# Places of their own for three of the steps that end a chunk, in slots 8 to 20 of a convolution, attention and experts kernel

## The chip, the core and the metric

The kernel runs on one core of one Trainium2 chip. The metric is the device time of one execution in microseconds. Before the change three executions took 3090.45, 3093.17 and 3100.2 us; the median is 3093.17 us.

The core has five engines with an instruction stream each: TensorE (PE, with its weight loads PEld), VectorE (DVE), ScalarE (ACT), GpSimd (POOL) and SyncE (SP, which issues most of the DMAs). [...]

## What is computed

The input is x of 8 images of 56 by 56 pixels with 256 channels, 8 x 3136 tokens in all. Three blocks follow each other (cut to what matters):

```python
# layer 0: 32 bottleneck paths, 256 -> 4 -> 3x3 -> 4 -> 256 channels, each with batch norm and relu
paths = vmap(_path)(x, W1, ..., V3)
x = relu(paths.sum(axis=0) + x)
# layer 1: attention without softmax; t has 8 heads of 32 channels
q = layernorm(t).heads
k = v = (q - mean) / (std(q, ddof=1) + 1e-5)      # per token and head
out = q @ (k.T @ v / N)                           # k.T @ v is 32 x 32, summed over all tokens of the image
t = t + out + layernorm(t)
# experts: top 2 of 8, gelu MLP 256 -> 256 -> 256
t = t + sum over e of combine[e] * (gelu(layernorm(t) @ w1[e] + b1[e]) @ w2[e] + b2[e])
```

What matters here is the middle: after the convolution of a chunk of tokens, their means and deviations per head are taken, the tokens are divided by the deviations, and the product k.T @ v is added to a sum that needs all chunks of its image before its attention can begin.

## The kernel before

**Chunks and slots.** The tokens are cut into S = 56 chunks of 448 (seven for each image), each laid out as 4 tiles of 112 tokens. The program is one long loop over slots. In slot s the heavy third convolution of chunk s runs, and woven into it are the lighter steps of other chunks: the first convolution of chunk s+2, the second of chunk s+1, the end of chunk s-1 (`end_steps`), and from slot A = 8 on the attention of chunk s-8. Routing of tokens to experts, the scattering of the routed rows to DRAM and the planning of expert tiles come with it. Expert tiles run from slot 18 on: a few in slots 18 to 20, and about as many as fit from slot 21 on, when the second plan is known (`known_in[1]` is 21).

**The third convolution** is 32 pairs a slot (`pair`): two matmuls into two PSUM banks (L660), a relu of the one on ACT into the tile `r` (L665), and a maximum and sum with the other on DVE (L668). A place of the order holds two such pairs; I call them PAIR0, PAIR2, ... PAIR30 by the number of the first. Two places, four pairs, make a unit, whose four `r` tiles are then summed over paths by TensorE (L681, `sum_paths`); these sums are SUM0 to SUM7, and SUM7 falls into the next slot. SUM5 takes the tiles of PAIR20 and PAIR22. Seven PSUM banks serve all matmuls but these sums, which have one bank, so that a pair may start only when ACT or DVE has read the banks of earlier ones.

**The end of a chunk** has ten steps: `begin` (relu, transposed copy to DRAM), `turn` twice (transposition on TensorE), `means` (DVE), `center` (POOL), `squares` (ACT), `variances` (ten DVE instructions, and at their end, L801, a power on POOL that turns variances into deviations), `inverse` (three DVE instructions, L814, L818, L823: the reciprocals of deviations, which read what the power wrote), `scale` (two POOL multiplications, L827), and `products` (16 matmuls, L837, and one DVE addition of the result, L845, or a copy, L843, in an image's first chunk).

**The order is written by hand.** PE, ACT and DVE execute in the order in which the program issues; POOL and SP are ordered when the program is built, by what is ready. `places` gives each step a place between 0 and 1 within the slot. `at` pairs steps with places, and `issue` sorts all steps of a slot by place and calls them. The third convolution is spread evenly over 0 to 1: a place of two pairs has weight 0.7 and a sum 0.9, together 18.4, so that PAIR22, which has 11 pair places and 6 sums ahead of it, stands at (7.7 + 5.4 + 0.35) / 18.4 = 0.731. In the same way PAIR20 stands at 0.644, SUM4 at 0.688, PAIR24 at 0.769, SUM5 at 0.812, PAIR26 at 0.856, PAIR28 at 0.894 and SUM6 at 0.938. Other steps near them are the second half of the second convolution with `halves` (DVE L340 and L342) at 0.675, the attention's writes of normalised rows on ACT (0.689, 0.744, 0.798, 0.881), its additive step on POOL (L1060, at 0.94) and, in slots with a plan (16 and 19), `runs` at 0.726 and `members` at 0.783, both on DVE.

Slots before 8 take the places of "end alone". All later ones up to 55 take those of "end".

Of the kernel before, what the change touches and what calls it, by code (L numbers as in the profile page):

```python
# [25 lines left out]
def kernel(  # L26
# [42 lines left out]
    A = NCH + 1  # L69
# [187 lines left out]
    def is_chunk(s):  # L257
        return 0 <= s < S
# [9 lines left out]
    def conv1_steps(s):  # L268
        b, c = divmod(s, NCH)
        xT = xtp.tile([P, NF, CH], F32, tag="xT", name=f"xT_{s}")  # L270
        xTs[s] = xT

        def turn(f):
            X = xs_in[s]
            tp = ps_mm.tile([P, 512], F32, tag="mm", name=f"tx_{s}_{f}")
            for k in range(KT):
                nc.tensor.transpose(
                    tp[:, k * T : (k + 1) * T], X[:, k, f * P : (f + 1) * P], ident[:T, :T]
                )
            nc.scalar.copy(xT[:, f, :], tp[:, :CH])  # L280

        def product():
            del xs_in[s]
            if is_chunk(s + 1):
                load(s + 1)
            ps = ps_mm.tile([P, 512], F32, tag="mm", name=f"c1_{s}")
            for f in range(NF):
                nc.tensor.matmul(
                    ps[:, :CH], W1s[:, f, :], xT[:, f, :], start=(f == 0), stop=(f == NF - 1)
                )  # L290
            nc.scalar.activation(
                h1[:, 1 + c * ROWS : 1 + (c + 1) * ROWS, 1 : HW + 1],
                ps[:, :CH].rearrange("p (r w) -> p r w", w=HW),
                AF.Relu, bias=sh1, scale=sc1,
            )

        return [(0.5, lambda: turn(0)), (0.5, lambda: turn(1)), (1.6, product)]
# [4 lines left out]
    def spread_taps(s):  # L302

        b, c = divmod(s, NCH)
        R = taps.tile([3 * 32, NG, TL], F32, tag="R", name=f"R_{s}")
        flat = h1.rearrange("p r w -> p (r w)")
        r0 = c * ROWS * W58
        for dx in range(3):
            n = TL - dx
            queue = nc.scalar if s == 0 and dx == 1 else nc.sync  # L310
            queue.dma_start(
                out=R[dx : 3 * 32 : 3, :, :n], in_=flat[:, r0 + dx : r0 + dx + n]
            )
        tapped[s] = R
# [174 lines left out]
    def center_router():  # L489
        tp = ps_mm.tile([P, 512], F32, tag="mm", name="tp_rw")  # L490
        for f in range(NF):
            nc.tensor.matmul(tp[:, :E], mean_of, rwc[:, f, :], start=(f == 0), stop=(f == NF - 1))
        for f in range(NF):
            nc.vector.tensor_sub(rwc[:, f, :], rwc[:, f, :], tp[:, :E])
# [109 lines left out]
    def unordered(ins, group, keep=()):  # L604
# [23 lines left out]
        "conv2": [0.621, 0.658, 0.658, 0.675],  # L628
        "conv2 alone": [0.531, 0.629, 0.629, 0.806],
        "end": [0.109, 0.151, 0.244, 0.244, 0.337, 0.431, 0.551, 0.681, 0.761, 0.908],  # L630
        "end alone": [0.121, 0.156, 0.166, 0.226, 0.306, 0.386, 0.386, 0.636, 0.73, 0.865],
        "fetch": [0.103],
        "image": [
# [58 lines left out]
    def conv3_steps(s):  # L692
        steps = []
        units = NF * NQ
        for step in range(0, 4 * units, 2):
            if is_chunk(s):
                steps.append((places["conv3"][0], lambda step=step: (pair(s, step), pair(s, step + 1))))
            if step == 0 and is_chunk(s - 1):
                steps.append((places["conv3"][1], lambda: sum_paths(s - 1, units - 1)))
            if step and step % 4 == 0 and is_chunk(s):  # L700
                steps.append((places["conv3"][1], lambda step=step: sum_paths(s, step // 4 - 1)))
        return steps
# [270 lines left out]
    def fetch(a):  # L973
        ts, tTs, us = spilled.pop(a)
        X = attn.tile([T, KT, C], F32, tag="X", name=f"X_{a}")
        tT = attn.tile([P, NF, CH], F32, tag="tT", name=f"tT_{a}")
        nc.sync.dma_start(out=tT, in_=tTs)
        nc.sync.dma_start(out=X, in_=ts)
        for n in range(2):
            nc.sync.dma_start(  # L980
                out=totals[a % 2][32 * n : 32 * n + 2, :].bitcast(F32), in_=us
            )
        fetched[a] = tT
        Xs[a] = X
# [541 lines left out]
    def at(name, steps):  # L1526

        out, last = [], 0.0
        for place, (_, fn) in zip(places[name], steps, strict=True):
            last = max(last, place)  # L1530
            out.append((last, last, [(0.0, fn)]))
        return out
# [20 lines left out]
    def tiles_by(s):  # L1553


        most = known_after[-2] - 2
        after = [int(v) for v in places["after"]]
        if s >= S:
            return most - sum(after[s - S + 1 :])
        begin, end = known_in[1] - 1, S - 1  # L1560
        at_hand = known_after[0] - 2
        return at_hand + (most - sum(after) - at_hand) * (s - begin) // (end - begin)


    def put_off(m):

        return m % NCH == NCH - 1 and m + 1 + A < S

    known_in = [
        m + A + 1 + (1 if m >= S - NCH else 2) + (1 if put_off(m) else 0) for m in closing  # L1570
    ]
    r, upto = -1, -2
    waiting, left = [], []
    for s in range(S + A + 1):
        a = s - A
        work_of = []
        era = " alone" if s < A else ""
        if s <= S:
            work_of.append((0.0, 1.0 if is_chunk(s) else 0.1, conv3_steps(s)))
        if is_chunk(s + 2):  # L1580
            work_of.extend(at("conv1" + era, conv1_steps(s + 2)))
        if is_chunk(s + 1):
            work_of.extend(at("taps" + era, [(0.0, lambda: spread_taps(s + 1))]))
            work_of.extend(at("conv2" + era, conv2_steps(s + 1)))
        if is_chunk(s - 1):
            if s < S:
                work_of.extend(at("end" + era, end_steps(s - 1)))
            else:
                work_of.append((0.12, 0.99, end_steps(s - 1)))
        if is_chunk(a + 1):  # L1590
            work_of.extend(at("fetch", [(0.0, lambda: fetch(a + 1))]))
        if is_chunk(a):
            opens = a % NCH == 0
            if opens:
                work_of.extend(at("image", image_steps(a // NCH)))
            if a + A > S:
                work_of.extend(at("attention first last" if opens else "attention last", attn_steps(a)))
            else:
                work_of.extend(at("attention first" if opens else "attention", attn_steps(a)))
        work_of.extend(left)  # L1600
        left = []
        group = waiting
        if waiting and put_off(waiting[0]):
            group = [] if waiting[0] == a - 1 else waiting[:1]
        if group and (len(group) == 2 or group[-1] % NCH == NCH - 1):
            last_image = group[-1] >= S - NCH
            compute, scatters = route_steps(group)
            rt = places["route" if s < S else "route last"]
            work_of.append((rt[0], rt[1], compute))
            if last_image:  # L1610
                work_of.append((places["scatter last"][0], 0.995, sum(scatters, [])))
            else:
                work_of.append((places["scatter"][0], 0.995, scatters[0]))
                left = [(0.0, places["scatter"][1], steps) for steps in scatters[1:]]
            if group[-1] in closing:
                work_of.append((places["plan"][0], places["plan"][1], plan_steps(closing.index(group[-1]))))
            waiting = waiting[len(group) :]
        while r + 1 < len(closing) and known_in[r + 1] <= s:
            r += 1
        if r >= 0 and r + 1 < len(closing):  # L1620
            goal = upto + (known_after[r] - 2 - upto) // (known_in[r + 1] - s)
            if r + 2 < len(closing):
                goal = min(known_after[r] - 2, goal if s < known_in[1] else tiles_by(s))
            work_of.append((places["tiles"][s <= known_in[r]], places["tiles"][2], moe_steps(upto, goal)))
            upto = goal
        if s == 1:
            center_router()
        if 1 <= s <= E:
            work_of.append((0.5, 0.5, [(0.0, lambda: copy_weights(s - 1))]))
            work_of.append((0.8, 0.8, [(0.0, lambda: empty_rows(s - 1))]))  # L1630
        if s == S + 1:
            apart.append(s)
        issue(*work_of)
        if is_chunk(a):
            waiting.append(a)
# [60 lines left out]
```

## Time and profile before

| what | us |
|---|---|
| three executions, median | 3093.17 |
| the profiled execution, from outside | 3074.19 |
| its span, first to last instruction | 3072.3 |
| PE busy | 2842.7 |
| DVE busy | 2143.1 |
| ACT busy | 1915.4 |
| POOL busy | 1798.8 |

The profile is of one execution, and all durations below are of that one. It was 19 us quicker than the median of the three; 1.9 us of it lie outside the span. The mean granted clock of TensorE was 0.968.

PE is busy for 93% of the span, but the share isn't even. The page's rows of 40 slices show it at 8 tenths in the part from about 307 to 845 us, which is that of slots 8 to 19 (slices of 76.8 us), and at 9 from there on. By the first matmul of the third convolution, slots start as follows.

| slot | starts at us | lasts us |
|---|---|---|
| 8 | 307.0 | 47.9 |
| 9 | 354.9 | 40.0 |
| 10 | 394.8 | 45.8 |
| 11 | 440.6 | 37.7 |
| 12 | 478.3 | 44.0 |
| 13 | 522.3 | 37.7 |
| 14 | 560.0 | 44.2 |
| 15 | 604.2 | 47.0 |
| 16 | 651.2 | 48.5 |
| 17 | 699.7 | 45.7 |
| 18 | 745.5 | 38.7 |
| 19 | 784.2 | 51.9 |
| 20 | 836.1 | 44.2 |

Slots 8 and 15 open an image's attention, 16 and 19 make a plan, and 10, 12, 14, 16, 17 and 19 route and scatter. A view of stretches gives each engine's busy time in such a window and the granted clock of TensorE; a view of the timeline gives the instructions in order with the idle time ahead of each and what ended it, in square brackets.

### The profile page before, as it was taken

What the parts mean: (1) busy time and instruction counts of PE and PEld (TensorE: products, weight loads), DVE (VectorE), ACT (ScalarE), POOL (GpSimd) and SP (SyncE); (2) the same over time, 40 slices, a digit from 0 to 9 for tenths busy, and PEclk for the clock granted to TensorE, in tenths of its full rate; (3) what the DMA queues carried; (4) which work ended last, traced back from release to release, by engine and by line L of the source; (5) the groups of instructions that cost most, each with busy time, mean ns of one, the idle gap of its engine ahead of it and who ended that gap; (6) DMA issues with size and microseconds to landing.
All of it is one profiled execution on the core that took longest, in us unless ns stands there. A gap on an engine that the chain in (4) does not pass through costs nothing.

```text
span 3072.3 us, 54367 instructions
## 1 busy us (share of the span) xinstructions
PE 2842.7 (93%) x16901; PEld 1649.8 (54%) x16901; DVE 2143.1 (70%) x5705; ACT 1915.4 (62%) x3859; POOL 1798.8 (59%) x1333
## 2 busy tenths in 40 slices
PE   7999888888899999999999999999999997898898
PEld 3334443334455555555555555555555555786687
DVE  6777878888777877787877877787778775453100
ACT  4666566556666676667766667667666664554355
POOL 2332245444565766757766666676664656677677
PEclk9999899989999999999999999999999998998899
DMA  3555445436477778677777877778877766998897
GB/s 102 145 118 131 113 141 137 130 103 183 122 179 190 172 200 209 164 199 188 195 193 176 207 175 190 195 176 206 193 167 185 182 175 147 230 278 215 208 215 172
DMA packets 373233, 538.19 MB, mean 175 GB/s; under 512 B 91488, under 2 KB 283344, under 8 KB 372944
## 3 DMA queue, kind: packets, MB, share of 16 engines
q1 hardware_dynamic: 289984, 430.49, 49.7%
q0 software_dynamic: 82368, 103.47, 20.3%
q8 instruction: 135, 2.21, 0.3%
q14 instruction: 154, 1.26, 0.2%
q10 hardware_dynamic: 592, 0.76, 0.1%
HBM read 248.42 MB, written 192.75 MB: 144 GB/s over the span
## 4 chain that ended last, share of the span: by engine, by line
PE 39%; DVE 4%; DMA 3%; ACT 3%; POOL 3%; issue 3%; POOLq 0%; ACTq 0%; DVEq 0%; SPq 0%
PE ph L1447 8%; PE py L1467 7%; PE c L660 6%; PE su L681 6%; DMA out_dram<-y,index 3%; PE te L1403 2%; PE py L1463 2%; PE at L1010 2%; PE c L324 2%; PE kv L837 1%; POOL regions L1191 1%; DVE r L668 1%; ACT r L665 1%; POOL out_dram L1485 1%; ACT y L1471 1%
## 5 line engine op out<-in xcount | busy, mean ns | idle before, releaser
L668 DVE SCALAR_TENSOR_TENSOR r<-c,nb,r 128x448 f32<-128x448 f32 x1792 | 1127.2, 676 | 379.1 <-ACT r L665 374.9
L665 ACT ACTIVATE r<-c,b3t 128x448 f32<-128x448 f32 x1792 | 1037.0, 634 | 340.7 <-PE c L660 334.5
L660 PE MATMUL c<-hl,W3hl 64*128 64x448 f32 x3584 | 700.7, 430 | 36.4 <-ACT r L665 19.8
L1191 POOL DMA_INDIRECT regions<-pay,rrowi x448 | 428.0, 955 | 300.0 <-PE c L660 181.5
L1485 POOL DMA_INDIRECT out_dram<-y,rows x258 | 408.0, 1582 | 318.4 <-ACT y L1471 243.1
L660 PEld LDWEIGHTS c<-hl,W3hl 64*128 64x128 f32 x3584 | 331.2, 188 | 488.9 <-issue 215.5
L681 PE MATMUL su<-r,gather 128*32 128x448 f32 x3584 | 540.5, 566 | 43.4 <-DVE r L668 33.6
L1471 ACT ACTIVATE y<-py,rows 128x256 f32<-128x256 f32 x420 | 195.9, 474 | 468.2 <-PE py L1467 348.0
L1447 PE MATMUL ph<-eT,w 128*128 128x256 f32 x1680 | 455.1, 402 | 18.6 <-ACT hT L1451 8.1
L1467 PE MATMUL py<-w,hT 128*128 128x256 f32 x1680 | 433.6, 383 | 0.0
L1447 PEld LDWEIGHTS ph<-eT,w 128*128 128x128 f32 x1680 | 301.6, 195 | 148.3 <-issue 30.3
L801 POOL TENSOR_TENSOR hsd<-hsd,half 112x36 f32<-112x36 f32 x49 | 302.4, 6171 | 99.8 <-DVE hsd L799 99.8
L754 POOL TENSOR_TENSOR norm<-t,hmean 112x512 f32<-112x512 f32 x112 | 115.6, 1058 | 354.9 <-DVE hmean L743 186.4
L1467 PEld LDWEIGHTS py<-w,hT 128*128 128x128 f32 x1680 | 292.0, 192 | 26.9
L1485 POOL DMA_INDIRECT out_dram<-y,index x162 | 251.0, 1549 | 94.1 <-issue 26.5
L1451 ACT ACTIVATE hT<-ph,w 128x256 f32<-128x256 f32 x420 | 197.1, 478 | 164.3 <-PE ph L1447 109.7
L681 PEld LDWEIGHTS su<-r,gather 128*32 128x32 f32 x3584 | 99.4, 109 | 231.2 <-DVE r L668 106.1
L1463 PE MATMUL py<-b2hl,own 128*128 128x256 f32 x420 | 175.1, 417 | 16.7 <-ACT y L1471 7.7
L1015 DVE SCALAR_TENSOR_TENSOR X<-at,rs,X 112x256 f32<-112x256 f32 x224 | 106.7, 476 | 98.0 <-PE at L1010 97.0
L1463 PEld LDWEIGHTS py<-b2hl,own 128*128 128x128 f32 x420 | 80.0, 190 | 145.4 <-issue 48.9
L324 PE MATMUL c<-R,W2t 96*32 96x448 f32 x1344 | 152.1, 555 | 2.5 <-ACT r L665 2.5
L1403 PE MATMUL te<-ident,rows 128*128 128x128 f32 x840 | 135.2, 284 | 19.4 <-ACT y L1471 18.4
(267 smaller groups left out, 3273.8 us busy)
## 6 DMA issues: line engine op xcount, KB each, us to landing
w<-Wd SPq DMA_DIRECT2D x210, 513.0 KB
rows<-regions SPq DMA_DIRECT2D x210, 259.0 KB
xi<-in_x_dram SPq DMA_DIRECT2D x56, 448.0 KB
hl<-hi SPq DMA_DIRECT2D x112, 224.0 KB
tTs<-xT SPq DMA_DIRECT2D x56, 448.0 KB
ts<-t SPq DMA_DIRECT2D x56, 448.0 KB
tT<-tTs SPq DMA_DIRECT2D x56, 448.0 KB
X<-ts SPq DMA_DIRECT2D x56, 448.0 KB
```

The source lines that it names most:

```text
L324: nc.tensor.matmul(ps[0][32 * g : 32 * g + 32, :CH], W2t[:, g, dy, :], R[:, g, :].rearrange("q (r w) -> q r w", w=W58)[:, dy : dy + ROWS, ...
L660: product = nc.tensor.matmul(tiles[g][:, :CH], W3hl[rows, ab, cg, :], hl[rows, ab, :], start=True, stop=True)
L665: nc.scalar.activation(r, tiles[0][:, :CH], AF.Relu, bias=b3t[:, cg, 2 * ab : 2 * ab + 1])
L668: nc.vector.scalar_tensor_tensor(r, tiles[1][:, :CH], nb3[:, cg, 2 * ab + 1 : 2 * ab + 2], r, op0=ALU.max, op1=ALU.add,)
L681: nc.tensor.matmul(ps[32 * c4 : 32 * c4 + 32, :CH], gather, unit.pop((s, 4 * u + c4)), start=(ab == 0), stop=(ab == NQ - 1),)
L801: nc.gpsimd.tensor_tensor(sd, sd, half[:T, :].rearrange("q (k h) -> q k h", k=KT), ALU.pow)
L1191: ins = nc.gpsimd.indirect_dma_start(out=regions[n], out_offset=bass.IndirectOffsetOnAxis(ap=v["row_i"][:, (m - group[0]) * KT + k, n : n ...
L1447: nc.tensor.matmul(ps, w[:, f * C + hf * P : f * C + (hf + 1) * P], eT[:, f, :], start=(f == 0), stop=(f == NF - 1),)
L1463: nc.tensor.matmul(ps, own.to_broadcast([P, P]), b2hl, start=True, stop=False)
L1467: nc.tensor.matmul(ps, hT[:, f, h * P : (h + 1) * P], w[:, (NF + f) * C : (NF + f + 1) * C], start=False, stop=(f == NF - 1),)
L1471: nc.scalar.activation(y[:, h, :], ps, AF.Identity, scale=g[:, h : h + 1])
L1485: ins = nc.gpsimd.indirect_dma_start(out=out_rows, out_offset=at, in_=y[:, h, :], in_offset=None, compute_op=ALU.add, **partial,).ins
```

## The change

A second list of places for the end of a chunk is added, and the slots from A = 8 to 20 use it. It differs from "end" in its last three entries: `inverse` moves from 0.681 to 0.741, `scale` from 0.761 to 0.771, and `products` from 0.908 to 0.92. No instruction is added or removed.

```diff
@@ -628,6 +628,7 @@
         "end": [0.109, 0.151, 0.244, 0.244, 0.337, 0.431, 0.551, 0.681, 0.761, 0.908],
+        "end first": [0.109, 0.151, 0.244, 0.244, 0.337, 0.431, 0.551, 0.741, 0.771, 0.92],
         "end alone": [0.121, 0.156, 0.166, 0.226, 0.306, 0.386, 0.386, 0.636, 0.73, 0.865],
@@ -1584,7 +1585,8 @@
         if is_chunk(s - 1):
             if s < S:
-                work_of.extend(at("end" + era, end_steps(s - 1)))
+                few = " first" if A <= s < known_in[1] else era
+                work_of.extend(at("end" + few, end_steps(s - 1)))
             else:
                 work_of.append((0.12, 0.99, end_steps(s - 1)))
```

## The prediction

> **What bounds the kernel now.** I first read the page's rows of slices, then the view of stretches cut at the slots' starts, because the change touches 13 slots alone. (The page's chain of waits can't help: followed back from the end, it doesn't reach this part.) Two slots side by side, with the columns length, busy us of PE, PEld, DVE, ACT and POOL, granted clock, DMA share and GB/s:
>
> ```profile
> 440.60:478.30 37.70, 33.00 (x209) 15.16 (x208) 30.46 (x67) 25.72 (x50) 20.98 (x15) 1.00 0.60 158
> 836.10:880.30 44.20, 43.97 (x276) 24.27 (x274) 31.05 (x67) 31.71 (x65) 30.66 (x22) 1.00 0.86 199
> ```
>
> Slot 20 (second row) has expert tiles: PE works 43.97 of 44.2 us, so a wait on another engine costs nothing there. Slot 11 (first row) has none: no engine is full. Its time is a chain of waits from engine to engine, and a stall on DVE can reach the end of the slot. The question is then who waits near `inverse`. The view of line L814 between 354.9 and 836.1 us, slots 9 to 19, says for how long and how often DVE stood idle before it:
>
> ```profile
>   POOL hsd L801: 21.2, 10
> ```
>
> DVE loses 2.25 to 2.30 us before L814 in each of slots 9 to 14, 17 and 18, and 1.51 in 16 and 19; in slot 15 (and in 8) nothing, since DVE comes there later than the power ends. In slot 20 it is 1.80, hidden. The timeline of slot 12 shows what this does (start, us, engine, line; in brackets the idle time before):
>
> ```profile
> 506.22 6.16 POOL L801 TENSOR_TENSOR hsd<-hsd,half 112x36 f32<-112x36 f32 x1 [0.58 <-DVE hsd L799]
> ...
> 509.40 1.16 ACT L665 ACTIVATE r<-c,b3t 128x448 f32<-128x448 f32 x2 [1.98 <-PE c L660]
> ...
> 509.49 0.62 DVE L342 TENSOR_TENSOR h<-h,hi 128x448 fp32r<-128x448 f32 x1
> ...
> 510.49 0.95 PE L681 MATMUL su<-r,gather 128*32 128x448 f32 x4
> ...
> 512.41 0.19 DVE L814 SCALAR_TENSOR_TENSOR hinv<-hsd 112x32 f32<-112x32 f32 x1 [2.30 <-POOL hsd L801]
> ...
> 512.95 2.42 DVE L668 SCALAR_TENSOR_TENSOR r<-c,nb,r 128x448 f32<-128x448 f32 x4
> ...
> 513.60 2.06 POOL L827 TENSOR_TENSOR norm<-norm,hinv 112x512 f32<-112x512 f32 x2
> ...
> 513.65 2.29 PE L681 MATMUL su<-r,gather 128*32 128x448 f32 x4 [2.21 <-DVE r L668]
> ...
> 515.88 1.29 PE L660 MATMUL c<-hl,W3hl 64*128 64x448 f32 x6
> ...
> 517.95 2.02 PE L837 MATMUL kv<-norm 112*128 112x129 f32 x16
> ```
>
> ACT has PAIR22 ready at 510.56, but DVE stands before L814 until the power is done at 512.38. PE does the half of SUM5 that needs PAIR20 (510.49 to 511.44) and then waits 2.21 us for PAIR22's `r`. PAIR26 follows, then `products` at 517.95, though `norm` was scaled at 515.66. That last distance, 2.29 us, is the lag I use below.
>
> **The change part by part.** Sorted by place, `inverse` goes behind SUM4, one ACT step and PAIR22; in slots 16 and 19 also behind the plan's `runs`, in 18 to 20 behind expert matmuls of PE and ACT. On DVE it is therefore moved past PAIR22's two L668, and those five instructions of `runs`, alone. `inverse` is three DVE instructions and issues no DMA. `scale`, two POOL instructions, goes past PAIR24, which has nothing on POOL or SP; the scatters at 0.778 and 0.865 stay behind it. `products` goes past nothing at all: no step stands between 0.908 and 0.92, and the next is SUM6 at 0.938. So the orders of PE and ACT stay as they are, and the whole effect is DVE's order, with what POOL makes of it.
>
> `inverse` moved, slot 12. DVE is free at 510.11 and takes PAIR22's two L668 (1.27 us a pair of them) from there to 511.4. It still waits for the power, now 1.0 us, and runs L814 at 512.41, as before: **the stall pays for the two instructions.** PAIR24 comes at 512.95 instead of 514.15. On PE, SUM5's second half follows the first at 511.45, PAIR26 at 512.4 instead of 515.88, and PAIR28, which needs a bank that PAIR24's L668 frees, ends at about 514.7. Then `products` waits for `scale`, which ends at 515.66 as before. **What is late next is the power itself:** power, reciprocals, scaling, products. The gain is min(lag, what PE gains), and here it's the lag.
>
> The lags, from the end of `scale` to the start of `products` in the timelines: slot 9 2.57, 10 1.96, 11 1.71, 12 2.29, 13 1.70, 14 1.26, 17 2.35, 18 2.71, together 16.5 us.
>
> Slots 16 and 19: `runs` takes 3.05 us (687.18 to 690.23). It moves under the wait of 1.51; PAIR22 then starts 2.1 us earlier (1.51 and the 0.6 of `inverse`), PE's waits of 5.20 and 3.43 before SUM5 shrink by as much, `scale` starts some 2.3 us later in slot 16 and still ends 3 us before `products` does now. I take 1.8 each, 3.6 together; the ends are 0 and 2.1.
>
> Slots 8 and 15: no wait before L814, so PAIR22 simply overtakes 0.6 us of `inverse`; in slot 8 PE waits 0.62 for it. `scale` ends 1.2 later, the lag is 1.55 and 1.71. I take 0.4 each, 0.8 together; ends -0.3 and 0.6. Slot 20: 0.
>
> [...] Slots 10 and 11 have the same stall of 2.2 us before SUM5, and this is the granted clock after it (columns: length, PE busy, clock, DMA share, GB/s):
>
> ```profile
> 431.00:433.00 2.00, 2.00 (x8) 0.62 0.15 46
> 433.00:435.00 2.00, 2.00 (x10) 0.50 0.00 0
> ...
> 469.00:471.00 2.00, 0.31 (x1) 1.00 1.03 329
> 471.00:473.00 2.00, 2.00 (x10) 1.00 0.22 80
> ```
>
> In slot 10 (the first two) it falls to half, and `products` takes 3.81 us instead of 2.02; in slot 17 2.96. Of the eight stalls of 2.2 us, half clock follows in slots 9, 10, 12, 17 and 18, not in 11, 13 and 14. [...] By the rule the slow stretches stay: PE gains no more than its 2.2 us before `products` (1.1 less than the lags of 9, 12, 17 and 18), so 15.4 + 3.6 + 0.8 = **19.8 us**. By the row the stall brings them, so they go: 16.5 + 3.6 + 0.8, and 1.8 and 0.9 for `products` at full clock in 10 and 17, **23.6 us**. As five of eight is neither always nor never, I take the middle, 21.7.
>
> Costs put at nothing: the power with DVE at work beside it (6.12 us in slot 8, where DVE never pauses, 6.13 in slot 11); the next chunk's `hl` DMAs, issued from 509.49, are over by 515 (DMA share 1.04 until then, 0.06 after), and the next slot now starts near 520. If they were late, the gain would end there. Of POOL's order the trace doesn't show the new one: already now the scatter at 0.778 runs before `scale` (512.58). One more costs 0.96 and 0.30 between issues, 1.26 us, in six slots (10, 12, 14, 16, 17, 19): from 0 to 7.6 us. I take 0, because the scatter at 0.865 waits for PAIR26 (513.1), when `scale` is due as well.
>
> Sum: 3074.2 - 21.7 = 3052.5 for the profiled execution (span 3050.6). The median shown is 19 us above that execution, for reasons outside the program, so I take the difference from it: 3093.2 - 21.7 = **3071.5 us**.
>
> **Rivals.** *A scatter gets in before `scale`*: 21.7 - 7.6 = 14, so 3079. For it: POOL is ordered by readiness, and PAIR26 gets ready earlier. Against: the tie is for `scale`. *Nothing to be measured*: gained time is lost again at the next wait, as in slot 20, where 1.80 us of DVE's waiting is hidden; 3091. Against: PE idles 4 to 9 us in each of slots 9 to 19 but a few tenths in slot 20. *Slower*: POOL puts L1060 (2.19 us, at 0.94) before `scale`. It waits for ACT's last row, in slot 11 until about 472, so that `scale` would end at 476.3 and `products` start 2.4 us later than today's 473.96; 9 such slots give 3115. It decides from the point where `scale` is due after ACT's last row; for it, the changed place itself, against it, that `scale` is due at 470.1, 2 us sooner.
>
> **Chances.** Forecast 0.65 (own range 3065 to 3078), scatter 0.15, nothing 0.12, slower 0.08. Measurements here tell a change from none at about 0.3%, 9.3 us. The first two cases are faster: 0.80; same 0.12; slower 0.08. Range: down to 3061, if slow clock stretches elsewhere in these slots go too (574.8 to 581.7 in slot 14 would give 3.4 us), up to 3088, over the scatter's case and the edge of no change; outside lie the slower case and most of no change.
>
> **To be seen afterwards.** Right: idle before L814 near 1 us in slots 9 to 14, 17 and 18; no wait of 2.2 us before SUM5; `products` within 0.3 us of the end of `scale`; those slots 1.3 to 4 us shorter; slots from 20 on as before. Wrong, if `scale` starts over 1 us later in these slots, if half clock still follows, or if a slot's gain is gone by the next slot's start.

## The result and the profile after

| what | before | after |
|---|---|---|
| five executions each, median us | 3093.53 | 3075.84 |
| their range | 3090.45 to 3100.2 | 3073.7 to 3079.05 |
| after / before, 95% interval | | 0.9937 (0.9923 to 0.995) |
| profiled execution, from outside | 3074.19 | 3075.17 |
| its span | 3072.3 | 3072.7 |
| slots 8 to 20 in the profile | 573.4 | 554.0 |
| slots 21 to 54 | 1636.8 | 1642.2 |
| start of slot 55 to the end | 555.2 | 568.9 |

The change makes the kernel 17.7 us faster by the medians; the interval of the ratio is 15 to 24 us. The two spans say nothing of it. The profile of before is of an execution 19 us below its own median, that of after is at its median. The two profiles also differ by 13.7 us after slot 55, where the programs issue the same work. On the chips of the experiments below, before takes 3075 to 3077 us, and the part after slot 55 takes 551.7 to 557.4 in all profiles taken there. So I read the change slot by slot, and such offsets drop out: slots 8 to 20 lose 19.4 us.

The first view is PE's groups of instructions in slots 9 to 19, where before spends 481.2 us and after 462.8. Columns: line, engine, operation, names, shapes, count, then busy us and mean ns, then the idle time ahead of the group and what ended it. Before:

```profile
L660 PE MATMUL c<-hl,W3hl 64*128 64x448 f32 x704 | 147.8, 450 | 16.8 <-ACT r L665 10.6 <-ACT lg L1019 3.6 <-DVE r L668 1.6
L681 PE MATMUL su<-r,gather 128*32 128x448 f32 x704 | 133.9, 587 | 35.3 <-DVE r L668 28.0 <-DVE xT L687 7.3
...
L837 PE MATMUL kv<-norm 112*128 112x129 f32 x176 | 25.1, 301 | 1.6 <-ACT r L665 0.7
```

After (lines from 632 on stand one lower, those from 1588 on two):

```profile
L661 PE MATMUL c<-hl,W3hl 64*128 64x448 f32 x706 | 151.7, 443 | 18.7 <-ACT r L666 11.2 <-ACT lg L1020 3.6 <-DVE r L669 1.4
L682 PE MATMUL su<-r,gather 128*32 128x448 f32 x704 | 128.3, 593 | 8.8 <-DVE xT L688 7.2 <-DVE r L669 1.4
...
L838 PE MATMUL kv<-norm 112*128 112x129 f32 x176 | 29.7, 326 | 5.3 <-POOL norm L828 4.6 <-ACT r L666 0.7
```

This is the account of the change. The sums' wait for DVE's L668 was 28.0 us and is 1.4: 26.6 us gone. Some of it comes back in `products`: 3.7 us more idle time, now for `scale`, and 4.6 us more busy time for the same 176 matmuls. The pairs (L661) take back 3.9 busy and 1.9 idle, and the sums are busy 5.6 less. Together that is about 18 of the 18.4 us by which these slots got shorter.

The view of the first reciprocal's line, L815, in slots 9 to 19 shows DVE's idle us and how often, where before had 21.2 us in ten:

```profile
  POOL hsd L802: 8.4, 8
```

That is 1.02 to 1.07 us in each of the eight slots, and nothing in 16 and 19. The timeline of slot 12 shows the new order. (Start, us, engine, line, operation; idle time in brackets. The prediction shows the same slot of before.)

```profile
500.57 6.16 POOL L802 TENSOR_TENSOR hsd<-hsd,half 112x36 f32<-112x36 f32 x1 [0.58 <-DVE hsd L800]
...
504.42 1.27 DVE L669 SCALAR_TENSOR_TENSOR r<-c,nb,r 128x448 f32<-128x448 f32 x2
...
504.84 1.85 PE L682 MATMUL su<-r,gather 128*32 128x448 f32 x8
...
506.77 0.19 DVE L815 SCALAR_TENSOR_TENSOR hinv<-hsd 112x32 f32<-112x32 f32 x1 [1.07 <-POOL hsd L802]
506.93 0.99 POOL L1192 DMA_INDIRECT regions<-pay,rrowi  x1 [0.20 <-PE su L682]
...
507.95 2.06 POOL L828 TENSOR_TENSOR norm<-norm,hinv 112x512 f32<-112x512 f32 x2
...
509.07 0.49 PE L838 MATMUL kv<-norm 112*128 112x129 f32 x2 [0.27 <-POOL norm L828]
510.07 2.91 PE L838 MATMUL kv<-norm 112*128 112x129 f32 x14 [0.51 <-POOL norm L828]
```

PAIR22's two L669 run under the power. SUM5's eight matmuls go through in one piece; before, a hole of 2.21 us split them. The reciprocals follow the power at once, and one scatter stands ahead of `scale`, as in before. In slots 8 to 20 of the two traces PE, ACT, POOL and SP each run the same instructions in the same order; DVE's order alone differs. What the prediction didn't have is in the last two lines. `products` starts 0.94 us before `scale` ends, since its first two matmuls need only the half of `norm` that is scaled first. It then waits 0.51 us for the other half, and takes 2.91 us for fourteen matmuls, which take 1.83 us at full clock (slots 9, 10, 13 and 14 of this profile). In the code the third to eighth matmul (`mine` with f = 0) read that first half too, so the wait is a dependency that the program sets and not a need of the data; doing without it wasn't tried. The slot lasts 44.2 us, as long as before (44.0), though its stall is gone.

The stretches of slots 11 and 20, which answer to the two rows of before in the prediction (length; busy us of PE, PEld, DVE, ACT, POOL; granted clock; DMA share; GB/s):

```profile
434.20:471.60 37.40, 34.62 (x209) 16.69 (x208) 30.35 (x67) 25.69 (x50) 21.34 (x16) 0.95 0.66 176
...
818.10:861.60 43.50, 43.28 (x275) 24.02 (x274) 31.13 (x67) 31.73 (x65) 30.68 (x22) 1.00 0.86 200
```

Slot 11 has 1.6 us more PE work than before (33.00) and a clock of 0.95, where before had 1.00: **a stretch of half clock has come into a slot that had none.** In slot 12 it is two. One lies upon `products`. The other begins 15.1 us into the slot, ahead of every instruction whose order changed; the second row is the same part of before (the first number is the length, the last four are as above):

```profile
486.67:493.49 6.82, 6.68 (x22) 0.50 0.08 24
...
493.40:500.20 6.80, 5.41 (x26) 1.00 0.09 25
```

Slot 17 has such an early stretch too (701.8 to 708.6, where before had full clock). By slots, in us:

| slots | predicted change | measured |
|---|---|---|
| 9 to 14, 17, 18 | -17.3 (middle of 15.4 and 19.2) | -12.1 |
| of these 9, 10, 13, 14 | | -2.8, -4.1, -1.8, -2.0 |
| of these 11, 12, 17, 18 | | -0.2, +0.2, -0.3, -1.1 |
| 16, 19 | -3.6 | -4.7, -2.6 |
| 8, 15 | -0.8 | -0.2, +0.9 |
| 20 | 0 | -0.7 |
| sum | -21.7 | -19.4 |

The total is close because a loss in one row and a surplus in another offset each other. The experiments are about both.

### The profile page after: what moved, and what is told of

Read it like the earlier page. It is cut to its first block, busy times and chain, and to the rows that moved or that the text cites. A ratio compares the mean times of both kernels' runs of the same rounds, so it can differ in the third digit from the quotient of the medians.

```text
span 3072.7 us, 54357 instructions
## 1 busy us (share of the span) xinstructions
PE 2850.7 (93%) x16901; PEld 1656.5 (54%) x16901; DVE 2143.9 (70%) x5705; ACT 1923.6 (63%) x3859; POOL 1801.4 (59%) x1333
## 3 DMA queue, kind: packets, MB, share of 16 engines
q0 software_dynamic: 82368, 103.47, 20.4%
q8 instruction: 135, 2.21, 0.3%
q14 instruction: 154, 1.26, 0.2%
## 4 chain that ended last, share of the span: by engine, by line
PE 43%; DVE 4%; issue 3%; ACT 3%; POOL 2%; DMA 1%; another core or an unknown queue 1%; POOLq 0%; ACTq 0%; DVEq 0%; SPq 0%
PE ph L1448 10%; PE py L1468 8%; PE c L661 7%; PE su L682 6%; PE te L1404 2%; PE py L1464 2%; PE at L1011 2%; PE c L324 2%; PE kv L838 2%; DVE r L669 1%; ACT r L666 1%; DMA out_dram<-y,index 1%; POOL hsd L802 1%; PE at L1007 1%
## 5 line engine op out<-in xcount | busy, mean ns | idle before, releaser
L669 DVE SCALAR_TENSOR_TENSOR r<-c,nb,r 128x448 f32<-128x448 f32 x1792 | 1126.8, 676 | 370.3 <-ACT r L666 325.2
L661 PE MATMUL c<-hl,W3hl 64*128 64x448 f32 x3584 | 705.8, 428 | 39.9 <-ACT r L666 20.0
L661 PEld LDWEIGHTS c<-hl,W3hl 64*128 64x128 f32 x3584 | 333.8, 187 | 493.4 <-issue 221.5
L1486 POOL DMA_INDIRECT out_dram<-y,rows x258 | 408.2, 1582 | 323.2 <-ACT y L1472 248.5
L682 PE MATMUL su<-r,gather 128*32 128x448 f32 x3584 | 534.2, 567 | 16.4 <-DVE xT L688 9.2
L1448 PE MATMUL ph<-eT,w 128*128 128x256 f32 x1680 | 460.2, 405 | 35.4 <-ACT hT L1452 13.6
L1486 POOL DMA_INDIRECT out_dram<-y,index x162 | 251.1, 1550 | 101.3 <-ACT y L1472 32.7
L1011 PE MATMUL at<-tab,tT 128*112 128x144 f32 x896 | 151.6, 293 | 0.1
```

What stands on the lines that cost most here:

```text
L661: product = nc.tensor.matmul(tiles[g][:, :CH], W3hl[rows, ab, cg, :], hl[rows, ab, :], start=True, stop=True)
L669: nc.vector.scalar_tensor_tensor(r, tiles[1][:, :CH], nb3[:, cg, 2 * ab + 1 : 2 * ab + 2], r, op0=ALU.max, op1=ALU.add,)
L682: nc.tensor.matmul(ps[32 * c4 : 32 * c4 + 32, :CH], gather, unit.pop((s, 4 * u + c4)), start=(ab == 0), stop=(ab == NQ - 1),)
L1011: nc.tensor.matmul(ps[:, f * P : f * P + WT], tT[:, f, k * T : (k + 1) * T], tab[:, f, :], start=False, stop=(f == NF - 1),)
L1448: nc.tensor.matmul(ps, w[:, f * C + hf * P : f * C + (hf + 1) * P], eT[:, f, :], start=(f == 0), stop=(f == NF - 1),)
L1486: ins = nc.gpsimd.indirect_dma_start(out=out_rows, out_offset=at, in_=y[:, h, :], in_offset=None, compute_op=ALU.add, **partial,).ins
```

## The experiments

Unless a diff says otherwise, only the list "end first" differs from the change; its last three numbers are the places of `inverse`, `scale` and `products`. Each ratio is to before on the same chip, with its 95% interval. The sum of slots 8 to 20 in a kernel's own profile is given in brackets (before 573.4, change 554.0).

**1. Which of the three moves does it?** Two kernels split the change.

```
-        "end first": [..., 0.741, 0.771, 0.92],
+        "end first": [..., 0.741, 0.761, 0.908],
```

> Of the three moved places only that of inverse is kept (0.741); scale and products stand where they did before (0.761, 0.908). Theory (DVE's wait for the power was on the slot's path, and the two L668 of PAIR22 now fill it): all of the gain is here, 16 to 20 us off the kernel before, ratio about 0.994, idle before the first instruction of inverse about 1.0 us in slots 9 to 14, 17 and 18. Rival (POOL's order, through the place of scale, or the place of products brings it): ratio 0.998 to 1.0.

```
-        "end first": [..., 0.741, 0.771, 0.92],
+        "end first": [..., 0.681, 0.771, 0.92],
```

> The complement: inverse stays at 0.681, scale goes to 0.771 and products to 0.92 in slots 8 to 20. Theory: products passes no step, scale passes only matmuls, so no change, within 0.2% of the kernel before, idle of 2.2 to 2.3 us before inverse in the eight slots as before. Rival (these two bring the gain): ratio about 0.994.

`inverse` alone: 3055.77 against 3076.98 us, 0.9927 (0.9908 to 0.9945) [553.8], and slot for slot the pattern of the change. `scale` and `products` alone: 3075.71 us, 0.9996 (0.9988 to 1.0005) [573.4], every slot within 0.05 us of before. All of the gain is DVE's order. The other two moves have no effect, since they change no engine's order: in slots 8 to 20 the traces show `inverse` alone with the orders of the change on all five engines, and `scale` and `products` alone with those of before. So these two kernels repeat the change and before.

**2. How much is there to have?** The kernel of before with the power left out in slots 8 to 20, so that nothing waits for it:

```
+            if A <= s + 1 < known_in[1]:
+                return
```

> The order of the kernel before, but the power on GpSimd (L801, 6.16 us) is left out in slots 8 to 20, so that there variances stand for deviations. Theory: DVE waits no longer before inverse (idle 0), the wait of 2.2 us of TensorE before SUM5 is gone, and products waits for nothing either, since the chain power, reciprocals, scaling is 6 us shorter: 18 to 27 us faster than before, at least what the change gains. Rival (the wait is hidden, and the gain of the change has another source): within 0.2% of the kernel before.

3047.54 us, 0.9913 (0.9898 to 0.9927) [544.7]. The power and the waits for it are worth 28.7 us in these slots (half clock falls from 88.7 to 68.3 us with them), and the change has two thirds of that. Slots 11 and 13 are 35.4 us long here, at clock 1.00. In the change, slot 13 has 35.9 but slot 11 has 37.5, so in slot 11 it isn't the power's own length that is missing.

**3. Are the waits inside `products` to blame?** They are PE's last small holes ahead of the new half clock (0.37 us in slots 11 and 18, 0.51 in 12 and 17). Here `products` goes behind SUM6, when all of `norm` is scaled:

```
-        "end first": [..., 0.741, 0.771, 0.92],
+        "end first": [..., 0.741, 0.771, 0.945],
```

> The changed kernel with products one step later in slots 8 to 20, at 0.945, behind SUM6. In the changed kernel TensorE begins products when the first half of norm is scaled and then waits inside it for the second. Theory (the end of scale is what TensorE waits for next): SUM6, 0.95 us, fills part of that wait, and half clock after it gets rarer: 5 to 10 us faster than the changed kernel, ratio to the kernel before about 0.991 to 0.992. Rival (the wait is paid at the next step anyway, or the later addition L845 holds DVE back): no different from the changed kernel, 0.9937, or slower.

3058.46 us, 0.9945 (0.9933 to 0.9957) [556.6]: not 5 to 10 us better than `inverse` alone, but 2.7 worse on the same chip, which the runs' spread doesn't tell from equal. The slots show two effects. Slots 11, 12, 13 and 18 do run at full clock (36.2, 41.5, 36.2 and 36.2 us; 13 did so before too), as the theory had it, but slot 19 takes 55.4 us (change 49.3) and slot 16 45.2 (change 43.8). So the next kernel keeps 0.945 only in the eight slots, and gives 8, 15, 16, 19 and 20 the places of the change:

```
+        "end plan": [..., 0.741, 0.771, 0.92],
...
+                if few == " first" and s in (8, 15, 16, 19, 20):
+                    few = " plan"
```

> The changed kernel with products at 0.945, behind SUM6, in slots 9 to 14, 17 and 18 alone; 8, 15, 16, 19 and 20 keep 0.92. Theory (what the traces of the change and of the last experiment show slot by slot adds up: SUM6 fills TensorE's wait inside products where there is one, and delays products where there is none): slots 8 to 20 take about 548.5 us against 554.0 in the changed kernel and 573.4 before; 5 us faster than the change on the same chip, ratio to the kernel before about 0.992. Rival (half clock windows only move from slot to slot): slots 8 to 20 take 553 us or more, no faster than the change.

3053.83 against 3074.59 us, 0.9925 (0.9912 to 0.9937) [553.4], not 548.5, and no faster than the change on the same chip (3048.01 us, below). The slots with the later place gain some 3 us over the change, and slot 19, whose own places are those of the change, loses 2.7: its half clock begins 14.8 us into the slot instead of 14.9, and lasts 13.7 us instead of 6.8. The rival held. That what is repaired in one slot shifts the next against the clock's changes is my reading of it.

**4. Further the same way.** `inverse` waits 1.0 us still, so I moved it behind PAIR24 as well:

```
-        "end first": [..., 0.741, 0.771, 0.92],
+        "end first": [..., 0.775, 0.78, 0.92],
```

> The changed kernel with inverse one pair place later still, at 0.775 behind PAIR24 (scale at 0.78), so that DVE has four L668 to do while the power runs and hardly waits. Theory (the 1.0 us that DVE still waits is no longer on the path; power, reciprocals, scaling is): idle before inverse falls to about 0, but inverse starts 0.3 us later in eight slots and about 1.2 us later in 16 and 19, so products comes no sooner: the same as the change or up to 5 us slower, ratio to the kernel before 0.994 to 0.996. Rival (DVE's remaining wait still costs): 6 to 9 us faster than the change, ratio 0.991 to 0.992.

3080.9 us, 1.0019 (1.0013 to 1.0026) [579.1]: slower than before, and 25 us worse than the change in these slots. Both theories missed. In seven of the eight slots DVE's wait is gone, and `inverse` comes only 0.42 to 0.46 us after the power (in slot 17 DVE waits 0.84). POOL's timeline in slot 12 of this kernel shows what that delay does:

```profile
506.67 6.16 POOL L802 TENSOR_TENSOR hsd<-hsd,half 112x36 f32<-112x36 f32 x1 [0.58 <-DVE hsd L800]
513.03 0.99 POOL L1192 DMA_INDIRECT regions<-pay,rrowi  x1 [0.20 <-PE su L682]
514.32 0.95 POOL L1192 DMA_INDIRECT regions<-pay,rrowi  x1 [0.30 <-issue]
515.57 0.94 POOL L1192 DMA_INDIRECT regions<-pay,rrowi  x1 [0.31 <-ACT r L666]
516.54 2.05 POOL L828 TENSOR_TENSOR norm<-norm,hinv 112x512 f32<-112x512 f32 x2
```

Three scatters stand between the power and `scale`, where the change has one. `scale` starts 9.87 us after the power's start, in the change 7.38. PE, which in the change waited some 0.8 us for it, waits long:

```profile
517.65 0.49 PE L838 MATMUL kv<-norm 112*128 112x129 f32 x2 [3.27 <-POOL norm L828]
518.64 3.38 PE L838 MATMUL kv<-norm 112*128 112x129 f32 x14 [0.51 <-POOL norm L828]
```

After 3.27 us of idle time half clock follows, 3.38 us for the fourteen matmuls. Slots that don't scatter (9, 11, 13, 18) are within 0.5 us of the change; 10, 12, 14, 16 and 17 lose 2.7 to 4.9 us each, and 19, with two scatters ahead of `scale`, 1.7. This is the rival "a scatter gets in before `scale`". It did not happen in the change and happens one place later, at more than its price. To test it, the same kernel with three of the eight scatters moved to the slot's end:

```
-            work_of.append((places["scatter"][0], 0.995, scatters[0]))
+            spots = [places["scatter"][0] + (0.995 - places["scatter"][0]) * (j + 0.5) / 8 for j in range(8)]
+            if s < known_in[1]:
+                spots[5:] = [0.985, 0.988, 0.991]
+            for p, step in zip(spots, scatters[0], strict=True):
+                work_of.append((p, p, [step]))
```

> The kernel with inverse at 0.775, which was slower than before, with one thing more: in slots 8 to 20 the last three of the eight scatters that a slot spreads from 0.302 to 0.995 stand at 0.985 to 0.991, so that none stands in POOL's order between the power and scale. Theory (that kernel lost its gain to scatters that got in before scale in 10, 12, 14, 16 and 17, where scale began 3 us after inverse): scale begins 0.75 us after inverse in all these slots, they take 41 to 42 us (10, 12, 14), 44 (16) and 45 (17), slots 8 to 20 take 551 to 556 us against 579 without it, ratio to the kernel before 0.991 to 0.994. Rival (the later inverse itself costs the 25 us): 570 us or more, ratio above 0.999.

3058.42 against 3076.54 us, 0.994 (0.9927 to 0.9953) [560.1]. No scatter stands between the power and `scale` any more, and 19 of the 25 us are back, so the scatters were the cause of those. The remaining 6 us missed the expectation. With its scatters as late (experiment 7), `inverse` at 0.741 takes 548.9 us in these slots, 11.2 less: the later `inverse` itself loses, as it puts `scale` 7.3 us after the power's start in all of the eight slots instead of 6.9.

**5. The same places in later slots.** For all of slots 8 to 55, then for seven chosen from that run:

```
-                few = " first" if A <= s < known_in[1] else era
+                few = " first" if A <= s else era
```

> The changed places in all slots from 8 to 55. From slot 21 on TensorE is full, and DVE waits 0.9 to 1.8 us before inverse in most slots. Theory (that wait is hidden there): slots 21 to 54 take 1636 us within 4 us, the whole within 4 us of the change on the same chip, ratio about 0.994. Rival (the wait is on the path in all slots): 0.5 to 1 us less in each of some 28 slots, 14 to 28 us more gain, ratio 0.985 to 0.990.

```
-                few = " first" if A <= s < known_in[1] else era
+                few = " first" if A <= s < known_in[1] or s in (22, 34, 41, 48, 50, 51, 54) else era
```

> The changed kernel with its places used in seven later slots too: 22, 34, 41, 48, 50, 51 and 54, which got shorter when all slots had them (by 0.4 to 2.6 us each, 8.6 in sum), while 21, 23, 24, 26, 28, 30 to 40 and 42 to 45 mostly got longer. Theory (a later inverse pays where POOL has no scatter to put before scale, with full TensorE too): slots 21 to 54 take 1627 to 1630 us against 1635.8, ratio 0.989 to 0.991, 5 to 8 us faster than the change on this chip. Rival (what one slot gains the next gives back): 1635 us or more, no faster than the change.

Everywhere: 3063.65 us, 0.9956 (0.9943 to 0.9969); slots 21 to 54 take 1645.2 us instead of 1636.8. Neither theory held: of these 34 slots 14 lose 0.6 to 1.2 us each, 33 and 40 lose 3.1 and 3.2, ten stay within 0.3, and eight gain 0.6 to 2.6 (22, 34, 41, 47, 48, 50, 51, 54; single profiles of other kernels differ by up to 1.6 us in 22 and 50, where nothing was changed). In 33 and 40 POOL has one more scatter and one more write of output rows (L1486) before `scale`, which starts 12.4 us after the power's start instead of 8.7. But it is as late in 21, 28, 35 and 42, which lose 1.1 us only, so the cause of these losses stays open. The seven slots alone: 3049.25 us, 0.9914 (0.9901 to 0.9927), with 1631.0 us in slots 21 to 54.

**6. The change again, twice.** In the first profile of the change, slots 25, 32, 39 and 46 had lost 0.9 to 1.6 us each, though nothing is changed in them. Does the change cost something later?

> The changed kernel once more, beside the others on one chip. In its first profile the stretch after slot 55 took 568.9 us, and 555 in the profiles of the kernel before and of the first two experiments, and four of the later slots lost 0.9 to 1.6 us each. Theory (the first profile is of another chip, on which the kernel before is slower too; the change does nothing after slot 20): that stretch takes 554 to 557 us here, slots 21 to 54 take 1635 to 1637, slots 8 to 20 554.0 as before, ratio 0.993 to 0.994. Rival (the change itself makes the later part slower, and gives back some of its gain): 565 us or more after slot 55 here too.

> The changed kernel beside these three on their chip, to compare with. Both theories: slots 8 to 20 take 554 us, 21 to 54 1636 if no slot stalls; ratio to the kernel before 0.991 to 0.994.

The first repeat: 3048.01 us, 0.9908 (0.9894 to 0.9923) [553.8], slots 21 to 54 in 1635.8; the later part isn't slower. Its profile is of the slowest of four executions, at 3055.47; the others took 3045.01 to 3048.51. The second: 3056.13 us, 0.9931 (0.9913 to 0.9949), with single executions from 3038.85 to 3062.62. Its profile is of the fastest of these, and slots 8 to 20 take **542.5 us** in it, 11.5 less than in the other profiles of the same order (554.0 in the first, 553.8 in the first repeat and in `inverse` alone). Half clock takes 51.2 us of them, instead of 81.9 (before 88.7). The 542.5 us are even below the 544.7 of the kernel without the power. Slot 11 shows the difference. The granted clock, which is 1.00 or 0.50 here, changes only at times that lie a multiple of 3.413 us apart, in each profile over all of slots 8 to 20. I cut the traces at those times and call the pieces windows. (Length, PE's busy time and count, granted clock, DMA share, GB/s.) The change's first profile:

```profile
459.41:462.82 3.41, 3.10 (x17) 1.00 0.98 89
462.82:466.24 3.42, 2.74 (x14) 1.00 0.68 227
466.24:469.65 3.41, 3.41 (x22) 0.50 0.22 60
```

The second repeat:

```profile
457.37:460.78 3.41, 3.09 (x18) 1.00 0.84 117
460.78:464.19 3.41, 2.74 (x16) 1.00 0.54 195
464.19:467.61 3.42, 3.42 (x31) 1.00 0.31 85
```

In each, the middle window has PE 2.74 us busy, 80%. In the one the next window runs at half clock, in the other it doesn't. The windows lie 0.3 us later against the slot's start in the second, and another part of `products` falls into them. With these windows the eight slots lose 18.5 us and slots 16 and 19 10.3, of 30.9 in all.

The record has each execution's mean granted clock. In the three kernels with the change's orders on the later chips (`inverse` alone and the two repeats), the seven executions of 3038.85 to 3048.51 us have 0.971 to 0.975, and the nine of 3055.47 to 3062.62 us have 0.965 to 0.969. In the first measurement of the change all five had 0.964 to 0.967. So the gain by medians, 17.7 us there and 20.4 to 26.6 elsewhere, depends on how many executions of each kind were caught.

The traces also show how the windows come to lie elsewhere. The first matmul of the program starts 0.2 to 3.3 us after an edge in the fourteen profiles (1.53 in that of before, 0.91 in the change's first). But the slots before 8, in which nothing is changed, fall into step with them: up to slot 7 half clock then comes once in two slots in all but one of the profiles, at times 68.3 us apart, which is twenty windows, and slot starts alternate. Here are the us from the last edge to the start of a slot:

| profile | slot 4 | 5 | 6 | 7 | 8 |
|---|---|---|---|---|---|
| the change, first | 0.82 | 1.21 | 0.74 | 1.18 | 1.81 |
| the change, second repeat | 1.24 | 0.78 | 1.21 | 0.73 | 2.27 |

In the other twelve profiles slots 6 to 8 have 0.7 to 0.8, 1.2 and 1.8 to 2.0 as well; the second repeat alone alternates the other way round.

**7. A version that beats both.** The change, with the seven later slots and the late scatters:

> The last one with the late scatters of slots 8 to 20 as well (inverse at 0.741). Theory (one scatter of 1.2 us still stands between the power and scale in 10, 12, 14, 16, 17 and 19, where scale begins 1.19 us after inverse): it begins 0.75 after, products 0.4 us sooner in each, 1 to 4 us less in slots 8 to 20, which take 550 to 553; together with the seven slots ratio 0.988 to 0.990, the fastest so far. Rival (half clock windows or scatters piled up at the slot's end take it back): slots 8 to 20 take 554 us or more.

**3036.55 us, 0.9874 (0.986 to 0.9888)** [548.9; slots 21 to 54: 1628.4], a little beyond the theory. That is 40 us less than before, and 19.6 less than the change on the same chip. POOL's timeline in slot 12 shows the late scatters:

```profile
499.40 6.16 POOL L802 TENSOR_TENSOR hsd<-hsd,half 112x36 f32<-112x36 f32 x1 [0.58 <-DVE hsd L800]
506.35 2.06 POOL L828 TENSOR_TENSOR norm<-norm,hinv 112x512 f32<-112x512 f32 x2 [0.78 <-DVE rs L824]
508.36 2.18 POOL L1061 TENSOR_TENSOR X<-X,pay 112x1024 f32<-112x1024 f32 x1
513.70 1.00 POOL L1192 DMA_INDIRECT regions<-pay,rrowi  x1 [3.16 <-PE c L661]
```

No scatter stands between the power and `scale`, which starts 6.95 us after the power's start instead of 7.38.

## Why the prediction was right, and where it was not

The forecast, -21.7 us, held against -17.7 by the medians and -19.4 by the slots. Its mechanism is shown: DVE's stall goes, and what is late next is the chain from the power. Several of its terms are not right, and that they sum to nearly the measured gain is luck.

- **DVE's order is the whole effect: right.** `inverse` alone has the whole gain, the two others none (experiment 1). As forecast, idle time before L815 is 1.02 to 1.07 us in the eight slots, the 2.2 us wait before SUM5 is gone, and POOL's order stays.
- **The clock term is what failed.** I took "the middle, 21.7" of 19.8 (slow stretches stay) and 23.6 (they go with the stall), for the eight slots 15.4 and 19.2. Measured are 12.1, under both ends. Where no half clock follows, the lags hold: 9, 10, 13 and 14 were to lose 9.3 us together (1.8 of it slot 10's clock) and lose 10.7. Slots 11, 12, 17 and 18 were to lose 10.0 (0.9 of it slot 17's clock) and lose 1.3: my own sign of being wrong, that half clock still follows, came there. The step assumed that a slow stretch comes with the stall, and goes or stays with it. In the traces it begins and ends at the edges of a grid of 3.413 us, and in slot 11 it came in one profile and not in the other, with PE 2.74 us busy in the window ahead in both. In these four slots only small waits of PE are left (0.26 to 0.51 us at `products`), and the slow stretch came upon `products` all the same, whose fourteen matmuls take 2.9 to 3.2 us there instead of 1.83; in 12 and 17 another came early in the slot. Slots 9, 10, 13 and 14 have waits of the same lengths and no slow stretch at `products`. Of half clock 81.9 us are left, of 88.7. In the second repeat, whose grid lies otherwise, these four slots lose 9.3 us, near the forecast. The lower end, 19.8 ("by the rule"), rests on slow stretches that stay when a stall of 2.2 us goes, a term that no run shows. What the runs showed in its place: of the five stretches that followed the stall, those of slots 9 and 10 went with it and those of 12, 17 and 18 stayed, and three came that before doesn't have, in 11 and early in 12 and 17.
- **"`products` within 0.3 us of the end of `scale`" was wrong in form.** It starts 0.80 to 0.95 us before that end, with the half that is ready, and waits inside. What is late next is nevertheless the chain that I named: power, reciprocals, scaling, products.
- **Slots 16 and 19 were undersized**: 1.8 each, 3.6 together, with an upper end of 2.1; measured are 4.7 and 2.6. Of `runs`, one instruction took 2.14 us beside `scale` and takes 0.18 where it stands now (last section), and in slot 16 PE's 5.20 us before SUM5 shrank to 1.15, and the half clock that followed (687.5 to 694.3) is gone as well.
- **Slots 8 and 15, 0.8 gain: missed**, 0.7 loss in sum. Slot 20, called hidden, gained 0.7 in every profile that has the changed order there.
- **The rivals.** "Scatter" was wrong for the change and right one place later (experiment 4), where I had priced it by POOL's 1.26 us a scatter; with the wait and the half clock that follow, it costs 2.7 to 4.9 us a slot. L1060 never got ahead of `scale`. "Nothing to be measured" and "slower" are outside the measured interval.

The sum was near by an offset: 5.2 us less than the middle in the eight slots and 1.5 less in 8 and 15, against 3.8 more in 16 and 19 and 0.7 more in 20.

Open: what decides which way round the slots fall into step with the clock's windows wasn't tried. That the other fast executions of the change are of the second repeat's kind is likely from their times and clocks, and not shown, since only the fastest has a profile. What brings the clock's step down is open too. Nor is it known why the first profile of the change lost time in slots 25, 32, 39 and 46 and after slot 55.

## What to carry to other kernels

Put the consumer of a long operation of another engine behind independent work on its own queue, and price the move by what is late next. Here the wait itself was 2.3 us, and the lag behind it, which bounds what PE can use, 1.3 to 2.7. Then look at the queue which takes over from it: 0.4 us of delay after the power let three ready scatters pass instead of one, and turned 20 us of gain into a loss. Where TensorE's clock changes on a fixed grid, as here at times 3.413 us apart, don't book a step down to a stall. A removed stall can bring half clock into slots that had none (slot 11 here, clock 0.95 instead of 1.00), so the lower bound must have room for that (here 12.1 us against a bound of 15.4), and a change is judged by several executions and by their clock.

## What the runs showed of the hardware

**A DVE instruction that ends with the POOL one beside it.** In slot 16 of before, the five instructions of `runs` follow `inverse` and meet `scale`. DVE and POOL in the timeline:

```profile
687.47 0.29 DVE L1289 TENSOR_REDUCE qx<-big 128x16 f32<-128x128 f32 x1
687.79 2.14 DVE L1290 TENSOR_TENSOR qi<-qx,q 128x16 f32<-128x16 f32 x1
689.85 0.16 DVE L1291 TENSOR_TENSOR start<-start,qx 128x16 f32<-128x16 f32 x1
```

```profile
687.83 2.06 POOL L827 TENSOR_TENSOR norm<-norm,hinv 112x512 f32<-112x512 f32 x2
```

After the change they run under the power (671.12 to 677.28):

```profile
676.37 0.18 DVE L1291 TENSOR_TENSOR qi<-qx,q 128x16 f32<-128x16 f32 x1
```

An addition of 16 elements per partition takes 2.14 us and ends 0.04 us after `scale`; under the power it takes 0.18 us. In slot 19 of before it is the same (822.88 to 825.02), and a small DVE operation of the attention (L1039, 0.15 us by its median) takes 1.16 to 2.02 us in four later slots, each ending within 0.06 us after `scale`. Why it is so beside `scale` and not beside the power isn't shown. The nearly 2 us were in my 3.05 us for `runs`, and I took them for its length.

**Half clock without a long wait.** Within slots 8 to 20 of the change, the window before each of the twelve steps down had PE busy for 58 to 80%, and of the 126 windows that no step followed all but two for 77% or more. In before that is less clear: 58 to 71% and 35 to 42% ahead of its thirteen steps, but twelve windows of 43 to 73% passed without one. So busy time as a trace models it doesn't decide alone, and a limit can't be given from it. One and the same order took 542.5 or 554.0 us in thirteen slots, in two profiles whose windows lie otherwise against the slots.
